# Router logits read out of the shared expert's product of rests

## The chip, the cores and the metric

The kernel runs on one core of one Trainium2 chip. The time is the device time of an execution in microseconds. A core has five engines with queues of their own: TensorE (PE in the profile, with its weight loads as PEld), VectorE (DVE), ScalarE (ACT), GpSimd (POOL) and SyncE (SP, used here to start DMAs). Each works through its own instructions in order; semaphores order them among each other. TensorE reads SBUF and writes PSUM, the accumulator memory, here in banks of 128 x 512 float32.

## The reference

One layer of a transformer over 64 batches of 128 tokens of 128 features: cross attention to 77 context tokens with 16 heads, then a feed-forward part with experts. Cut to what matters here:

```python
x = x + xattn(layernorm(x), ctx)              # 16 heads of 64, 77 keys
x2 = layernorm(x).reshape(-1, 128)            # 8192 tokens
logits = x2 @ router_w.T                      # 8 experts
_, idx = top_k(softmax(logits), 2)
gate = zeros; gate[token, idx] += logits[token, idx]
for e in range(8):
    h = silu(x2 @ w1[e].T) * (x2 @ w3[e].T)   # 176 wide
    moe_out += gate[:, e:e+1] * (h @ w2[e].T)
sh = silu(x2 @ sw1.T) * (x2 @ sw3.T)          # the shared expert, 176 wide
x = x + moe_out + sh @ sw2.T
```

All data are float32. The width 176 of an expert is worked as a main part of 128 and a "rest" of 48.

## The kernel before

The 64 batches are worked in 16 groups of 4 (512 tokens). Attention runs in units: one unit is one batch with 8 of the 16 heads, so a group has 8 units. The main loop over the 128 units issues for each: the scores of the unit two ahead (`ps`, whose two PSUM banks exist once, so the next scores wait until DVE has read the last: `mx`, `sc`), every second unit the output product `py`, then a list of work that is due at an even step, the transposes `pa` of this unit's attention weights, ACT's exponentials for the unit ahead, the values `pv`, a list due at an odd step, and last DVE's sums `sm`, `ri` and POOL's products `at`, which the transposes two units later read. Each unit thus has two steps and a group 16. Key products `pk` are due at each step. In odd groups of attention four products `pn` are due too, at steps 2, 4, 6 and 8.

The plan (`at(when, ...)`, lines 935 to 946) also places the routing of a group, in the 16 steps behind its attention: layer norm statistics at step 0, scaling at 1, transposing at 3 (`pxT_f`, copied by ACT to `x2T`), logits at 4, choice of the first expert at 5 and of the second at 6, places in the experts' lists at 8, and from 9 to 12 eight indirect DMAs by POOL that send the tokens (`sent`). A group's routing runs while the next group is in attention. "Odd" and "even" groups are those of the routing: while an even group is routed, an odd group is in attention, with `pn`.

For the first 13 groups (the last `LATE` = 3 are worked at the end) the shared expert stands in the same plan: up products of the main parts at step 11 (`p_s`, two products of 512 columns), the rest at 12, the down products at 14 (`pf`) and the storing at 17. The rest is one product, `ph_s`, of 112 weight columns: 0 to 47 are the first matrix, 64 to 111 the third, and 48 to 63 are zero. ACT takes a tanh of its first 48 rows, and DVE makes the gated rest `hr` of it in two instructions, `ur` and `hr`, that read the product in PSUM (lines 520 to 523).

Logits (lines 552 to 564) are four products, one a batch, of 128 weight columns (the batch's tokens in `x2T`) and 8 streamed columns (`rw_sb`), followed by a copy to SBUF on DVE, a maximum and a difference there, and an exponential on ACT. `choose` is nine small DVE instructions, `choose_second` seven with `sel`; `place` starts with products `pr` that read `sel`.

From step 160 on, the blocks of chosen tokens run between the units: sets of 9, 5 and 2 groups are sent and then worked in "quads" of four blocks, with copies of the experts' weights `w` on ACT and DVE, transposes `pt`, up products `p` and `ph`, down products `pq`, and indirect DMAs `answers`. Their gating uses the same functions, `gated` and `gated_rest`. PSUM banks other than those of the scores are six in a ring (`bank`). Every engine's instructions keep the order in which the recording layer leaves them.

Of the kernel before, what the change touches and what calls it, by code (L numbers as in the profile page):

```python
# [8 lines left out]
F32 = mybir.dt.float32  # L9
# [6 lines left out]
B, NQ, D = 64, 128, 128  # L16
# [10 lines left out]
E, I = 8, 176  # L27
IR = I - 128
HI = 64 + IR

W1, W3, WR, W2F, W2R, WALL = 0, 128, 256, 256 + HI, 384 + HI, 512 + HI
G = 4
NG = B // G

SETS = (9, 5, 2)

LATE = 3
# [8 lines left out]
def n_blocks(n):  # L46
    return 2 * n * G * NQ // 128 + E - 1

# [4 lines left out]

T = G * NQ
EPS = 1e-5
# [13 lines left out]
def xattn_moe_kernel(  # L69
# [9 lines left out]
    wvT: bass.AP,  # L79
    w_out: bass.AP,  # L80
    b_out: bass.AP,
    rwT: bass.AP,
    wx: bass.AP,
    wsh: bass.AP,
    out: bass.AP,
# [1 line left out]
    nc = tc.nc  # L87
    PSUM = bass.MemoryType.PSUM

    const = ctx.enter_context(tc.tile_pool(name="const", bufs=1))  # L90
# [8 lines left out]
    ffn = ctx.enter_context(tc.tile_pool(name="ffn", bufs=2))  # L99
    per_set = ctx.enter_context(tc.tile_pool(name="per_set", bufs=2))  # L100

    def weights_of(engine, w, q, n, name):

        to = ffn.tile([128, WALL], F32, tag="w", name=f"{name}_{q}", bufs=2 * QUAD)
        to = to[:, : 4 * n].rearrange("p (m d) -> p m d", d=n)
        engine.dma_start(out=to, in_=w[:, 4 * q : 4 * (q + 1), :])
        return to

    wk, wq, wv, wo = {}, {}, {}, {}
    for q in range(2):  # L110
        wq[q] = weights_of(nc.scalar, wqT, q, D, "wq")
        wk[q] = weights_of(nc.sync, wkT, q, DC, "wk")
    mhalf = const.tile([128, G], F32, name="mhalf")
    nc.gpsimd.memset(mhalf, -0.5)

    nc.scalar.activation(small.tile([128, G], F32, tag="shift", name="first_exp"), mhalf, AF.Exp)

    def load_keys(g):
        cT = grp.tile([DC, G, NKV], F32, tag="cT", name=f"cT_{g}", bufs=2)
        nc.sync.dma_start(out=cT, in_=ctxT[:, g * G : (g + 1) * G, :])  # L120
        return cT
# [30 lines left out]
        wv[q] = weights_of(nc.scalar, wvT, q, DC, "wv")  # L152
        wo[q] = weights_of(nc.sync, w_out, q, D, "wo")
    bo_sb = const.tile([128, D], F32, name="bo_sb")
    rw_sb = const.tile([D, E], F32, name="rw_sb")
    wsh_sb = const.tile([128, WALL], F32, name="wsh_sb")

    wx_sb = const.tile([128, E, WALL], F32, name="wx_sb")
    nc.scalar.dma_start(out=bo_sb, in_=b_out.rearrange("(o d) -> o d", o=1).broadcast_to([128, D]))
    nc.sync.dma_start(out=rw_sb, in_=rwT)  # L160
    nc.sync.dma_start(out=wsh_sb, in_=wsh)

    def load_expert(e):
# [6 lines left out]
    ident = const.tile([128, 128], F32, name="ident")  # L170
# [3 lines left out]
    for i in range(NAT):  # L174
        a = const.tile([128, 8 * (KM + KS)], F32, name=f"at_{i}")
# [60 lines left out]
    def bank(name, p=128):  # L236
        return ps_g.tile([128, 512], F32, tag="g", name=name)[:p]
# [230 lines left out]
    def wide(a, shape):  # L468

        return a.rearrange("p (b o) -> p b o", o=1).broadcast_to(shape)  # L470
# [17 lines left out]
    def gated(name, up, silu=False, n=T):  # L488

        p1 = bank(f"p1_{name}")  # L490
        up(p1, W1, 128)
        p3 = bank(f"p3_{name}")
        up(p3, W3, 128)
        a = ffn.tile([128, T], F32, tag="a", name=f"a_{name}")
        h = ffn.tile([128, T], F32, tag="h", name=f"h_{name}", bufs=3)
        of = slice(0, n)
        if silu:
            nc.scalar.activation(a[:, of], p1[:, of], AF.Silu)
            nc.vector.scalar_tensor_tensor(h[:, of], a[:, of], 2.0, p3[:, of], ALU.mult, ALU.mult)
        else:  # L500

            nc.scalar.activation(a[:, of], p1[:, of], AF.Tanh, scale=0.5)
            u = ffn.tile([128, T], F32, tag="u", name=f"u_{name}")
            nc.vector.scalar_tensor_tensor(u[:, of], a[:, of], 1.0, p1[:, of], ALU.add, ALU.mult)
            nc.vector.tensor_tensor(h[:, of], u[:, of], p3[:, of], ALU.mult)
        return h

    def gated_rest(name, up, silu=False, n=T):

        pr = bank(f"ph_{name}")  # L510
        up(pr, WR, HI)
        a = ffn.tile([128, T], F32, tag="a", name=f"ar_{name}")
        hr = hrs[hr_no[0] % NHR]
        hr_no[0] += 1
        of = slice(0, n)
        if silu:
            nc.scalar.activation(a[64:HI, of], pr[:IR, of], AF.Silu)
            nc.vector.scalar_tensor_tensor(hr[:IR, of], a[64:HI, of], 2.0, pr[64:HI, of], ALU.mult, ALU.mult)
        else:
            nc.scalar.activation(a[:IR, of], pr[:IR, of], AF.Tanh, scale=0.5)  # L520
            u = ffn.tile([128, T], F32, tag="u", name=f"ur_{name}")
            nc.vector.scalar_tensor_tensor(u[64:HI, of], a[:IR, of], 1.0, pr[:IR, of], ALU.add, ALU.mult)
            nc.vector.tensor_tensor(hr[:IR, of], u[64:HI, of], pr[64:HI, of], ALU.mult)  # L523
        return hr

    class Router:
# [23 lines left out]
            nc.scalar.copy(self.pay[:, 1, :, :D], self.pay[:, 0, :, :D])  # L550

        def logits(self):
            pl = bank(f"pl_{self.g}")
            for b in range(G):
                nc.tensor.matmul(
                    pl[:, b * E : (b + 1) * E], self.x2T[:, b * NQ : (b + 1) * NQ], rw_sb, start=True, stop=True
                )
            self.lg = lg = self.t3("lg")
            nc.vector.tensor_copy(lg.rearrange("p b e -> p (b e)"), pl[:, : G * E])
            m = self.t2("gm")  # L560
            nc.vector.tensor_reduce(m, lg, AX.X, ALU.max)
            self.sc = sc = self.t3("gsc")
            nc.vector.tensor_tensor(sc, lg, wide(m, sc.shape), ALU.subtract)
            nc.scalar.activation(sc, sc, AF.Exp)
# [90 lines left out]
        def up(self, to, c, m):  # L655
            nc.tensor.matmul(to[:m], wsh_sb[:, c : c + m], self.x2T, start=True, stop=True)  # L656

        def shared_up(self, silu=False):
            self.h = gated(f"s{self.g}", self.up, silu)
# [200 lines left out]
    def at(when, *steps):  # L860
        plan.setdefault(when, []).extend(steps)
# [42 lines left out]
    for g in range(NG):  # L904
        p = 16 * g
# [15 lines left out]
    def route(g, step, *args):  # L921
        if g not in routers:
            routers[g] = Router(g, next(s for s in sets if s.start <= g < s.start + s.n), atts[g].x1)
        getattr(routers[g], step)(*args)

    def routing(g, p, *steps):
        for k, step in steps:
            at(p + k, lambda step=step: route(g, step))

    g = 0  # L930
# [3 lines left out]
    assert g == NG  # L934
    for g in range(NG - 1):
        p = 16 * (g + 1)
        routing(g, p, (0, "stats"), (1, "normed"), (3, "transpose"), (4, "logits"), (5, "choose"), (6, "choose_second"))
    for st in sets:
        for g in range(st.start, min(st.start + st.n, NG - 1)):
            p = 16 * (g + 1)  # L940
            routing(g, p, (8, "place"))
            if g < NG - LATE:
                routing(g, p, (11, "shared_up"), (12, "shared_rest"), (14, "shared_down"), (17, "park"))
            for k in range(4):
                for c in range(2):
                    at(p + 9 + k, lambda g=g, c=c, b=k: routers[g].send(c, b))
    end = 16 * NG
    for st in sets[:-1]:
        p = 16 * (st.start + st.n)
# [6 lines left out]
    for st, after in zip(sets, sets[1:]):  # L956
# [4 lines left out]
        for q, quad in enumerate(quads):  # L961
            p = st.ready + (until - st.ready) * q // (len(quads) - 1)
# [109 lines left out]
    def unit(k):  # L1072
        g, b, t = units[k]
        return attention_of(g), b, t
# [28 lines left out]
    for k in range(len(units) + 1):  # L1103
# [3 lines left out]
        if k and k % 2 == 0:  # L1107
            a, b, t = unit(k - 1)
# [4 lines left out]
        a, b, t = unit(k)  # L1113
# [24 lines left out]
def _laid_out(inputs):  # L1138

    import numpy as np  # L1140

    a = {k: np.asarray(v) for k, v in inputs.items()}
    f = np.float32

    def packed(w1, w3, w2):

        w = np.zeros((128, WALL), f)
        w[:, W1:W3] = w1[:128].T
        w[:, W3:WR] = w3[:128].T
        w[:, WR : WR + IR] = w1[128:].T  # L1150
        w[:, WR + 64 : W2F] = w3[128:].T
        w[:, W2F:W2R] = w2[:, :128].T
        w[:IR, W2R:] = w2[:, 128:].T
        return w

    keys = a["ctx_768"].transpose(2, 0, 1)
    ctxR = np.zeros((DC, B, KS), f)
    ctxR[:, :, :KR] = keys[:, :, KM:]
    ctxM = keys[:, :, :KM].reshape(DC, B // 2, 2 * KM)
    ctxM = np.concatenate([ctxM, ctxM[:, :, :KM]], axis=2)  # L1160

    def by_pair(w):

        return w.reshape(NH // 2, 128, -1).transpose(1, 0, 2)

    w1, w2, w3 = (a[f"L0_ffn_w{n}"] for n in (1, 2, 3))
    return {
        "x": a["x"],
        "xT": a["x"].transpose(2, 0, 1),
        "ctxT": keys,  # L1170
        "ctxM": ctxM,
        "ctxR": ctxR,
        "wqT": by_pair(a["L0_xattn_w_q"].T),
        "wkT": by_pair(a["L0_xattn_w_kv"][:, :INNER].T),
        "wvT": by_pair(a["L0_xattn_w_kv"][:, INNER:].T),
        "w_out": by_pair(a["L0_xattn_w_out"]),
        "b_out": a["L0_xattn_b_out"],
        "rwT": a["L0_ffn_router_w"].T,
        "wx": np.concatenate([packed(w1[e], w3[e], w2[e]) for e in range(E)]),
        "wsh": packed(a["L0_ffn_sw1"], a["L0_ffn_sw3"], a["L0_ffn_sw2"]),  # L1180
    }


# [17 lines left out]
```

## Time and profile before

| what | us |
|---|---|
| median of 3 runs | 972.41 (971.56 to 974.22) |
| the profiled execution | 973.28 |
| its span | 971.6 |
| TensorE busy | 921.3 (95%) |
| VectorE busy | 668.8 (69%) |
| ScalarE busy | 653.0 (67%) |
| GpSimd busy | 520.2 (54%) |
| logits products, TensorE busy | 15.3 in 128 instructions |
| product of rests of the shared expert, TensorE busy | 16.4 in 32 instructions |

The span runs from the first to the last instruction of the profiled execution; 1.7 us lie around it. A product of float32 is recorded as two instructions, one a pass, and a transpose as one. Records of TensorE overlap[...]: what an instruction takes from the queue is read from the distance of two starts. In a group of instructions the line gives engine, operation, output and inputs with shapes, the count, then busy time in all and the mean of one in ns, then the idle time of the engine in front of them and what ended it. In the chain that ended last, each line is a start, a duration and the instruction.

### The profile page before, as it was taken

The numbers are of one execution on the slowest core, as the hardware profiler recorded it, in microseconds if no ns is written. First come the engines' busy times: TensorE is split into PE (matmuls) and PEld (weight loads), VectorE is DVE, ScalarE is ACT, GpSimd is POOL, SyncE is SP. The second block draws the span as 40 slices with busy tenths as digits, with TensorE's granted clock in tenths as the row PEclk, the third lists the DMA queues.
The fourth block names the chain that finished last, engine by engine and source line by source line (L and its number), as shares of the span: only waits on it lengthen the run. The fifth ranks groups of instructions, "written<-read, shape, count | busy, mean of one in ns | idle before, by whom it ended". The sixth has DMA issues, their size and how long they took to land.

```text
span 971.6 us, 18867 instructions
## 1 busy us (share of the span) xinstructions
PE 921.3 (95%) x6123; PEld 768.4 (79%) x6123; DVE 668.8 (69%) x1751; ACT 653.0 (67%) x1420; POOL 520.2 (54%) x688
## 2 busy tenths in 40 slices
PE   8999999999999999999999999999999988879794
PEld 7787878788778778787898878888888877779692
DVE  4566776777667667768787576777676787656464
ACT  5776667676767676676767685767766766576461
POOL 3244553636364636545457556475465483646773
PEclk9999999999999999999999999999999999999898
DMA  6222212222221232122403322221322032424886
GB/s 181 70 57 78 68 41 82 67 59 67 68 83 43 63 104 59 54 82 69 110 23 99 96 83 67 54 72 56 93 75 70 15 96 88 124 65 110 259 255 225
DMA packets 80882, 85.76 MB, mean 88 GB/s; under 512 B 11328, under 2 KB 62912, under 8 KB 80784
## 3 DMA queue, kind: packets, MB, share of 16 engines
q1 hardware_dynamic: 65920, 56.09, 21.4%
q0 software_dynamic: 8864, 18.30, 5.6%
q10 hardware_dynamic: 6000, 10.16, 2.9%
q8 instruction: 49, 0.80, 0.3%
q14 instruction: 49, 0.40, 0.1%
HBM read 48.18 MB, written 36.33 MB: 87 GB/s over the span
## 4 chain that ended last, share of the span: by engine, by line
PE 72%; DVE 10%; ACT 9%; DMA 4%; issue 3%; SPq 1%; ACTq 0%; POOL 0%; POOLq 0%; DVEq 0%
PE py L446 13%; PE ps L367 11%; PE pk L350 11%; PE pv L419 8%; PE pa L436 5%; PE p L784 5%; PE pn L456 2%; PE pq L797 2%; PE p_s L656 2%; PE pq L796 2%; PE ph L784 2%; DVE sm L389 1%; DVE sc L378 1%; ACT y L803 1%; PE pf L669 1%
## 5 line engine op out<-in xcount | busy, mean ns | idle before, releaser
L350 PEld LDWEIGHTS pk<-cT,wkq_sb 96*128 96x128 f32 x1024 | 157.9, 189 | 70.0 <-issue 42.8
L357 ACT COPY kx<-pk 128x308 f32<-128x308 f32 x256 | 104.3, 416 | 129.0 <-PE pk L350 123.5
L807 POOL DMA_INDIRECT answers<-y,to x149 | 149.4, 1003 | 72.4 <-ACT y L803 29.0
L350 PE MATMUL pk<-cT,wkq_sb 96*128 96x154 f32 x1024 | 175.0, 294 | 1.0 <-ACT wkq_sb L267 0.7
L446 PEld LDWEIGHTS py<-vo,aT 128*128 128x128 f32 x1280 | 154.7, 193 | 14.4 <-ACT vo L424 3.9
L367 PE MATMUL ps<-kx,xgT 128*128 128x308 f32 x512 | 156.7, 426 | 9.8 <-DVE sc L378 9.3
L446 PE MATMUL py<-vo,aT 128*128 128x128 f32 x1280 | 157.0, 277 | 3.0 <-ACT vo L424 2.6
L645 POOL DMA_INDIRECT sent<-pay,row x128 | 126.7, 989 | 61.5 <-DVE part L635 30.9
L399 POOL TENSOR_TENSOR at<-sc,ri 128x512 f32<-128x512 f32 x64 | 67.2, 1051 | 171.0 <-DVE ri L391 113.7
L424 ACT COPY vo<-pv 64x512 f32<-64x512 f32 x256 | 147.1, 574 | 2.1 <-ACT vn L464 0.4
L419 PE MATMUL pv<-wvo_sb,cM 96*128 96x512 f32 x256 | 131.2, 594 | 1.0 <-DVE hr L523 0.8
L389 DVE TENSOR_REDUCE sm<-sc 128x8 f32<-128x616 f32 x128 | 101.1, 790 | 40.1 <-ACT sc L382 39.2
L382 ACT ACTIVATE sc<-sc,rs_a 128x616 f32<-128x616 f32 x128 | 104.9, 820 | 25.9 <-DVE sc L378 16.9
L367 PEld LDWEIGHTS ps<-kx,xgT 128*128 128x128 f32 x512 | 88.9, 189 | 39.0 <-issue 8.9
L397 POOL TENSOR_TENSOR at<-sc,ri 128x256 f32<-128x256 f32 x128 | 76.8, 624 | 79.2 <-DVE ri L391 25.2
L439 ACT COPY aT<-pa 128x512 f32<-128x512 f32 (+1 forms) x256 | 96.1, 429 | 32.0 <-PE pa L436 27.3
L378 DVE TENSOR_TENSOR sc<-ps,mx 128x616 f32<-128x616 f32 x128 | 102.3, 800 | 12.5 <-POOL at L401 0.4
L376 DVE TENSOR_REDUCE mx<-ps 128x8 f32<-128x616 f32 x128 | 98.3, 768 | 7.7 <-PE ps L367 6.4
L436 PE MATMUL pa<-ident,at 128*128 128x128 f32 x640 | 91.7, 274 | 0.2 <-POOL at L397 0.2
L436 PEld LDWEIGHTS pa<-ident,at 128*128 128x128 f32 x640 | 75.2, 142 | 11.6 <-issue 10.7
L784 PE MATMUL p<-xT,w 128*128 128x128 f32 x596 | 75.2, 280 | 8.4 <-ACT xT L779 8.3
L784 PEld LDWEIGHTS p<-xT,w 128*128 128x128 f32 x596 | 71.0, 194 | 12.9 <-ACT xT L779 11.4
(152 smaller groups left out, 1402.6 us busy)
## 6 DMA issues: line engine op xcount, KB each, us to landing
xb<-sent SPq DMA_DIRECT2D x149, 65.0 KB
last_values<-vn ACTq DMA_DIRECT2D x32, 256.0 KB
vo<-last_values SPq DMA_DIRECT2D x64, 128.0 KB
ya<-answers SPq DMA_DIRECT2D x15, 512.0 KB
xgT<-in_xT_dram SPq DMA_DIRECT2D x16, 256.0 KB
xg<-in_x_dram SPq DMA_DIRECT2D x16, 256.0 KB
parked<-x SPq DMA_DIRECT2D x14, 256.0 KB
yx<-parked SPq DMA_DIRECT2D x14, 256.0 KB
```

Source lines behind the costliest of these rows:

```text
L350: nc.tensor.matmul(pk[:, k].rearrange("p (b k) -> p b k", k=NKV), wkq_sb[:, 2 * i + k, :], self.cT[:, 2 * p : 2 * (p + 1), :], start=True, ...
L367: nc.tensor.matmul(ps[:, r, : 4 * NKV].rearrange("p (j k) -> p j k", k=NKV), self.xgT[:, ts], self.kx[p][:, h : h + 4, ks], start=True, st ...
L378: nc.vector.tensor_tensor(at, sc, over_keys(mx), ALU.subtract)
L382: nc.scalar.activation(at, at, AF.Exp, scale=self.norm.rs[:, b : b + 1])
L389: nc.vector.tensor_reduce(sm, at, AX.X, ALU.add)
L419: nc.tensor.matmul(pv, self.cM[:, p, KM * r : KM * (r + 2)], wvo_sb[:, h : h + 4, :], start=True, stop=True)
L424: nc.scalar.copy(self.vo[b][rows, 4 * t : 4 * (t + 1), :], pv[rows].rearrange("p (m d) -> p m d", d=D))
L436: nc.tensor.transpose(pa[:, j * NQ : (j + 1) * NQ], keys[:, c : c + 128], ident)
L446: nc.tensor.matmul(py[:, :D], aT[:, m, :], vo[:, m, :], start=(m == 0), stop=(m == NT - 1))
L645: ins = nc.gpsimd.indirect_dma_start(out=sent[st.i], out_offset=bass.IndirectOffsetOnAxis(ap=self.row[:, i : i + 1], axis=0), in_=self.pay ...
L784: nc.tensor.matmul(to[:m, ts], self.w[j][:, c : c + m], self.xT[:, ts], start=True, stop=True)
L807: ins = nc.gpsimd.indirect_dma_start(out=answers[st.i], out_offset=bass.IndirectOffsetOnAxis(ap=self.to[:, j : j + 1], axis=0), in_=self.y ...
```

## The change

For the first 13 groups the logits come out of the shared expert's product of rests. The router's 8 weight columns are laid into the zero columns 48 to 55 of that product's weights, in the array `wsh` that the host lays out; the array `rwT` and its load go. The product `ph_s` moves from step 12 to step 4. ACT copies it whole, 112 x 512, from PSUM to a new SBUF tile `rests`. At step 5, four transposes of 128 tokens each turn the 112 rows into columns in one bank, and `weigh` (the rest of the former `logits`) reads columns 48 to 55 of each. `choose` moves from step 5 to 6 and `choose_second` from 6 to 7. At step 12 the tanh and the two DVE instructions read `rests` instead of the product in PSUM. For the last three groups logits are computed as before, with the weight columns from `wsh`. The tile `h` of the gating has two buffers instead of three.

```diff
+WG = WR + IR
...
-    rw_sb = const.tile([D, E], F32, name="rw_sb")
+    rests = const.tile([HI, T], F32, name="rests")
...
-    nc.sync.dma_start(out=rw_sb, in_=rwT)
...
-        h = ffn.tile([128, T], F32, tag="h", name=f"h_{name}", bufs=3)
+        h = ffn.tile([128, T], F32, tag="h", name=f"h_{name}", bufs=2)
...
     def gated_rest(name, up, silu=False, n=T):
-        pr = bank(f"ph_{name}")
-        up(pr, WR, HI)
+        if up is None:
+            pr = rests
+        else:
+            pr = bank(f"ph_{name}")
+            up(pr, WR, HI)
...
         def logits(self):
-            pl = bank(f"pl_{self.g}")
+            pl = bank(f"pl_{self.g}")[:, : G * E].rearrange("p (b e) -> p b e", e=E)
             for b in range(G):
                 nc.tensor.matmul(
-                    pl[:, b * E : (b + 1) * E], self.x2T[:, b * NQ : (b + 1) * NQ], rw_sb, start=True, stop=True
+                    pl[:, b, :], self.x2T[:, b * NQ : (b + 1) * NQ], wsh_sb[:, WG : WG + E], start=True, stop=True
                 )
+            self.weigh(pl)
+
+        def product_of_rests(self):
+            pr = bank(f"ph_s{self.g}")
+            self.up(pr, WR, HI)
+            nc.scalar.copy(rests, pr[:HI])
+
+        def logits_of_rests(self):
+            pl = bank(f"pl_{self.g}").rearrange("p (b e) -> p b e", b=G)
+            for b in range(G):
+                nc.tensor.transpose(pl[:, b, :HI], rests[:, b * NQ : (b + 1) * NQ], ident[:HI, :HI])
+            self.weigh(pl[:, :, IR : IR + E])
+
+        def gated_rests(self):
+            self.hr = gated_rest(f"s{self.g}", None)
+
+        def weigh(self, pl):
             self.lg = lg = self.t3("lg")
-            nc.vector.tensor_copy(lg.rearrange("p b e -> p (b e)"), pl[:, : G * E])
+            nc.vector.tensor_copy(lg, pl)
...
-        routing(g, p, (0, "stats"), (1, "normed"), (3, "transpose"), (4, "logits"), (5, "choose"), (6, "choose_second"))
+        routing(g, p, (0, "stats"), (1, "normed"), (3, "transpose"))
+        if g < NG - LATE:
+            routing(g, p, (4, "product_of_rests"), (5, "logits_of_rests"), (6, "choose"), (7, "choose_second"))
+        else:
+            routing(g, p, (4, "logits"), (5, "choose"), (6, "choose_second"))
...
-                routing(g, p, (11, "shared_up"), (12, "shared_rest"), (14, "shared_down"), (17, "park"))
+                routing(g, p, (11, "shared_up"), (12, "gated_rests"), (14, "shared_down"), (17, "park"))
...
+    shared = packed(a["L0_ffn_sw1"], a["L0_ffn_sw3"], a["L0_ffn_sw2"])
+    shared[:, WG : WG + E] = a["L0_ffn_router_w"].T
```

More of the change, by code (lines that the diff above doesn't have):

```diff
@@ L81, in xattn_moe_kernel @@
     b_out: bass.AP,
-    rwT: bass.AP,
     wx: bass.AP,
@@ L1177, in _laid_out @@
         "b_out": a["L0_xattn_b_out"],
-        "rwT": a["L0_ffn_router_w"].T,
         "wx": np.concatenate([packed(w1[e], w3[e], w2[e]) for e in range(E)]),
-        "wsh": packed(a["L0_ffn_sw1"], a["L0_ffn_sw3"], a["L0_ffn_sw2"]),
+        "wsh": shared,
     }
```

## The prediction

> **What bounds the kernel now.** First the page's head and the busy times, then the busy times of two stretches: attention and routing alone (50 to 430 us), and the stretch in which the experts' blocks run between attention units (columns: stretch, length, then busy us and instruction count of PE, PEld, DVE, ACT, POOL, granted clock, DMA share, GB/s).
>
> ```profile
> span 971.6 us, 18867 instructions
> ...
> PE 921.3 (95%) x6123; PEld 768.4 (79%) x6123; DVE 668.8 (69%) x1751; ACT 653.0 (67%) x1420; POOL 520.2 (54%) x688
> ```
>
> ```profile
> 50.00:430.00 380.00, 379.46 (x2328) 303.28 (x2327) 268.10 (x758) 264.85 (x571) 191.49 (x262) 1.00 0.22 65
> 480.00:850.00 370.00, 352.44 (x2463) 302.25 (x2462) 268.89 (x684) 253.24 (x563) 215.39 (x264) 1.00 0.26 75
> ```
>
> TensorE is the bound: 379.46 of 380 us at full clock, and 352 of 370 with experts. So what the change takes from TensorE's queue is a gain at its full issue time, unless another engine then makes TensorE wait. DVE is 71% busy and next. Third, the groups of instructions that the change removes or resembles (busy us, mean ns of one, then idle before and its releaser).
>
> ```profile
> L555 PE MATMUL pl<-rw_sb,x2T_f 128*128 128x8 f32 x128 | 15.3, 246 | 0.0
> L318 PE MATMUL pxT_f<-ident,pay 128*128 128x128 f32 x64 | 9.7, 274 | 0.0
> L320 ACT COPY x2T_f<-pxT_f 128x512 f32<-128x512 f32 x16 | 9.5, 591 | 0.0
> L564 ACT ACTIVATE gsc<-gsc 128x32 f32<-128x32 f32 x16 | 3.7, 230 | 24.7 <-DVE gsc L563 24.7
> ```
>
> Two things to see: the 64 logits products are 128 instructions (two passes each), the 64 transposes are 64 (one pass each); and ACT stands 24.7 us in all, 1.54 a time, in front of the router's exponential. Fourth, the chain that ended last, in order of time, over the router of group 3.
>
> ```profile
> 205.83 0.44 PE pxT_f L318 x4
> ...
> 210.25 0.81 PE pl L555 x8
> 211.09 0.20 DVE lg L559
> ...
> 213.80 0.19 DVE oh L574
> 213.99 0.71 DVE sm L389
> ...
> 215.70 0.80 DVE sc L378
> ...
> 216.65 1.28 PE ps L367 x4
> ...
> 231.82 0.86 PE ph_s L656 x2
> ```
>
> The four logits products hold TensorE for 0.81 us (the same distance, 0.81 to 0.82, stands behind all 16 of them in the timeline). Then, in this odd group, the chain leaves TensorE: logits, choice of the first expert, sm, mx, sc on DVE, and the next scores wait for sc. TensorE's previous product issued at 215.85 and takes 0.52, so it was ready at 216.37 and began at 216.65: 0.28 lost. Groups 1, 5 and 7 show 0.27 at the same place; even groups, which have an extra pn product there, lose nothing.
>
> **The change, part by part.** It touches 13 of the 16 groups.
>
> *1. Logits by transpose.* Removed: 4 products, 0.81 us. Added: 4 transposes of 112 columns. The nearest row is pxT_f, 4 transposes of 128 columns in 0.44; the five of pa take 0.54 (210.90 to about 211.45 in the timeline), the same 0.11 each. With 112 of 128 columns this is 0.38 if the streamed columns set the pace, 0.44 if the load of 128 columns does; I take 0.40. The Trainium skill ("TensorE: Matmul & The Clock Gate", Part 4: PE-mode transpose) speaks against this: it gives some 275 ns for one transpose in a kernel's context, so four would be 1.10 and the change would lose 0.29 x 13 = 3.8 us. The row has a mean of 274 ns too, but that is the length of one record: starts lie 0.11 apart because they overlap. I take the distance, so 13 x (0.81 - 0.40) = **-5.3** (4.8 to 5.6).
>
> *2. The product of rests (ph_s), 0.86 us, moves* from step 12 to step 4. It is not doubled, so the sum on TensorE is zero; between the steps the queue runs 0.86 + 0.40 - 0.81 = 0.45 later than before, afterwards 0.41 earlier. Its DMAs: none. The transposes wait for ACT's copy of it. Between product and transposes TensorE issues pa 0.54, pv 0.86 and pk 0.52 = 1.9 us; the copy (row x2T_f: 0.59, here 112 rows) needs about 0.15 + 0.59. Cover 1.2 us, and ACT is free there: it used to wait at this very place for the exponential. Where the cover is gone, TensorE stands for the difference, with the next scores behind.
>
> *3. ACT: 13 copies more*, 7.7 us busy. They fill the wait for the exponential, which moves to the end of the unit, behind aT, exp, vo and kx copies, by when DVE has its input. aT copies in group 3 begin at 211.75 instead of 211.90. Cost nothing; with ACT late, aT and kx would be late next, then py and scores. The tanh at step 12 no longer waits for ph_s (5.4 us in all by the waits), hidden, since DVE there has slack.
>
> *4. DVE: choose (9 small instructions, 2.0 us) moves a unit later*, so steps 4 and 5 carry 3 of them, steps 6 and 7 carry 16. Walk of group 3: transposes issue 212.88 to 213.28, lg at 213.47, gsc done 214.1, sm, ri, mx, sc to 216.61, next scores from 216.76; TensorE, 0.46 later, comes at 216.79. The 0.28 is then spent working: the odd groups gain it, 4 x 0.26 = **-1.0** (0 to -1.1). Then choose and second until 220.1, where pr needs sel at 220.66; sm, ri, mx, sc of the next unit to 222.65, wanted at 222.75. Margins of 0.5 and 0.1: that is the tight place. `place` comes at 222.9 instead of 220.84, so POOL's sends are 2.1 us later; its at tiles for units 6 and 7 are ready about 2.2 and 0.8 us before pa wants them. Even groups: pn's 0.86 gives slack, place is only 0.42 later.
>
> *5. Groups 9 to 12, between experts' blocks.* The exponential's waits there are 1.4 to 2.8 us of ACT; freeing them brings xT and the blocks' hr forward, and TensorE's waits just after the logits are 0.33, 0.35, 0.52 and 0.98 (xT or hr): of 2.2 I take **-1.0** (0 to -2.2). Against it, group 9: choose filled a DVE gap at 492.4 to 494.4; later it ends second at 504.2, and pr, at 503.4 in the queue, waits: **+0.85** (0 to 1.5).
>
> *6. The gate reads SBUF.* ur and hr now have two SBUF inputs (0.68 and 0.69, as before from PSUM). The skill ("SBUF — State Buffer", Who interferes with whom) says that such an instruction and a GpSimd instruction that reads SBUF exclude each other. This trace agrees: a pair of small products with two SBUF inputs, 0.29 elsewhere, took 1.59 under POOL's at.
>
> ```profile
> 504.68 1.59 DVE L623 SCALAR_TENSOR_TENSOR picked<-oh,place 128x32 f32<-128x32 f32 x2
> ```
>
> ```profile
> 504.83 1.06 POOL L399 TENSOR_TENSOR at<-sc,ri 128x512 f32<-128x512 f32 x1
> ```
>
> By the old row the two gates cost nothing; by the rule up to one at (0.62 to 1.06) each, 13 x 2 x 1.06 = 27 us if nothing hid it. In even groups POOL works on at and x through 279.1 to 281.9, where ur and hr run: about 0.9 later, hr done near 282.2, pf wants it at 282.35. In odd groups POOL is sending then. I take 0.05 a group, **+0.7** (0 to 4).
>
> *7. At nothing:* h in 2 buffers instead of 3 (no third up product stands ahead of the down product two blocks earlier in TensorE's order); one load less at the front of SP's queue; the router's columns inside wsh; banks (ph is freed after 0.75 us instead of 3).
>
> Sum: -5.3 - 1.0 - 1.0 + 0.85 + 0.7 = -5.75, say -5.8. The profiled execution took 973.28 (span 971.6, 1.7 around): 967.5. It lies 0.87 above the median of 972.41, so the forecast against the median is **966.6**.
>
> **Rivals.** (a) *DVE eats the gain.* Steps 6 and 7 hold 6.2 us of DVE (16 x 0.22, mx, sc, sm, ri) against a TensorE unit of some 4 us; if the margins 0.1 and 0.5 fall by 0.3 to 0.5, each group stalls that much at scores or pr: 13 x 0.4 = 5.2 given back, 971.8. For it: the margins; against it: the unit before is lighter by 2.0.
> (b) *Slower, by one mechanism: the gates of step 12 and POOL lock each other,* hr comes late at pf and sm, mx, sc behind it come late at scores. Each full at that DVE meets costs 1.06; with one per gate, 2.1 less a slack of some 0.5 leaves 1.6 x 13 = 20.8, less 6.45 (the sum without item 6) = +14.4: 986.8. It decides from 6.45/13 = 0.5 us a group for no change, 0.72 for 0.3% slower. For it: the 1.59 above. Against: sends, not at, lie there in odd groups. If it comes it is likelier near its point of decision, 976 to 980.
> (c) *The transposes are no cheaper* (two passes each, 0.8): 972.4 - 0.5 = 971.9. The x64 and x640 for 64 and 640 transposes speak against it.
>
> **Chances.** A change of 0.3% (2.9 us) is about what a measurement can tell. Main case 0.64 (own range 963.0 to 969.4), (a) 0.17, (b) 0.13, (c) 0.03, the rest (0.03) faster than 963 by more waits removed. So faster 0.67, same 0.20, slower 0.13. The range takes in the main case's bounds and (a) and (c) nearly whole: 962.5 to 974.5.
>
> **What would show it.** Right: 52 transposes pl, some 0.40 from the first to the next instruction; the exponential's wait on ACT near 5 us instead of 24.7; scores after step 5 of odd groups without a gap; TensorE's busy stretch unbroken to 430. Wrong: TensorE waiting for sel (pr), for sc (scores) or for hr (pf) in groups 0 to 8; ur or hr longer than 1 us; transposes 0.8 apart; new waits of POOL's at on DVE with pa behind them.

## The result and the profile after

The changed kernel takes 978.88 us (median of 6 runs, 977.14 to 981.29), the kernel before, run beside it, 972.86 (971.56 to 974.22): a ratio of 1.0054, 95% interval 1.004 to 1.0068. It is slower by 0.5%, where 966.6 (962.5 to 974.5) was forecast. Its profiled execution took 978.02.

The page's head and busy times of the changed kernel, and then its busy times in the two stretches that were shown of before:

```profile
span 976.3 us, 18778 instructions
...
PE 918.6 (94%) x6071; PEld 763.4 (78%) x6071; DVE 687.2 (70%) x1751; ACT 660.4 (68%) x1433; POOL 527.4 (54%) x688
```

```profile
50.00:430.00 380.00, 374.12 (x2273) 297.26 (x2271) 272.69 (x745) 265.26 (x569) 194.41 (x259) 1.00 0.22 65
480.00:850.00 370.00, 351.84 (x2438) 300.22 (x2436) 276.29 (x673) 258.90 (x572) 215.77 (x263) 1.00 0.26 75
```

TensorE's work fell by 2.7 us of record time, but from 50 to 430 us, where it had stood still for 0.54 us, it now stands still for 5.88. DVE is busy 18.4 us longer with the same number of instructions. Which ones, the groups of instructions say; first the gate's two in the kernel before, then those that the change added or altered:

```profile
L522 DVE SCALAR_TENSOR_TENSOR ur_s<-ar_s,ph_s 48x512 f32<-48x512 f32 x13 | 8.8, 681 | 5.3 <-ACT ar_s L520 5.2
L523 DVE TENSOR_TENSOR hr<-ur_s,ph_s 48x512 f32<-48x512 f32 x13 | 9.0, 690 | 0.4
```

```profile
L525 DVE SCALAR_TENSOR_TENSOR ur_s<-ar_s,rests 48x512 f32<-48x512 f32 x13 | 27.7, 2131 | 0.5
L526 DVE TENSOR_TENSOR hr<-ur_s,rests 48x512 f32<-48x512 f32 x13 | 13.9, 1072 | 0.4
L567 ACT COPY rests<-ph_s 112x512 f32<-112x512 f32 x13 | 7.6, 586 | 5.4 <-PE ph_s L677 5.4
L572 PE MATMUL pl<-ident,rests 112*128 112x112 f32 x52 | 7.1, 259 | 0.0
L585 ACT ACTIVATE gsc<-gsc 128x32 f32<-128x32 f32 x16 | 3.7, 232 | 7.3 <-DVE gsc L584 7.3
```

`ur_s` takes 2.13 us in the mean (0.70 at least, median 3.08, 3.42 at most) where it took 0.68, `hr` 1.07 where it took 0.69: together 23.8 us more in 13 groups, which is more than the whole rise of DVE. The transposes came out as forecast, and the exponential's wait nearly so (24.7 us before, 7.3 now, about 5 forecast). In the chain that ended last, group 3 now begins so:

```profile
215.48 0.40 PE pl L572 x4
215.88 0.02 issue
215.91 0.20 DVE lg L580
...
218.26 0.80 DVE sc L378
219.06 0.10 DVE gs L601
```

0.40 for the four transposes, where the four products held TensorE for 0.81. Now the gate of an even group (4) in the timelines of DVE, POOL and TensorE, in this order:

```profile
282.21 3.09 DVE L525 SCALAR_TENSOR_TENSOR ur_s<-ar_s,rests 48x512 f32<-48x512 f32 x1
285.34 0.69 DVE L526 TENSOR_TENSOR hr<-ur_s,rests 48x512 f32<-48x512 f32 x1
```

```profile
282.01 1.20 POOL L397 TENSOR_TENSOR at<-sc,ri 128x256 f32<-128x256 f32 x2
283.16 0.38 POOL L401 TENSOR_TENSOR at<-sc,ri 128x104 f32<-128x104 f32 x1
283.49 1.26 POOL L339 TENSOR_TENSOR x<-xg,bo_sb 128x512 f32<-128x512 f32 x1
284.91 1.28 POOL L666 DMA_INDIRECT sent<-pay,row  x1 [0.16 <-issue]
```

```profile
284.47 0.39 PE L689 MATMUL pf<-wsh_sb,h_s 128*128 128x128 f32 x2
286.08 0.49 PE L690 MATMUL pf<-wsh_sb,hr 128*128 128x128 f32 x2 [1.22 <-DVE hr L526]
```

POOL began 0.2 us earlier, and its four products and sums follow each other without a gap until 284.75. `ur_s` ends at 285.30, which is 0.55 behind the last of them: DVE stood through the whole run, not through one instruction (this standing is called the lock below), and the down product `pf` waits 1.22 us for `hr`. Beside the indirect DMA `sent`, which POOL issues next, `hr` takes its usual 0.69.

Where the time went along the kernel is read from the starts of the 128 scores `ps` in TensorE's timeline: start before minus start after, so positive is gained. The last column is an experiment told below, in which only the gate's lock is taken away.

| stretch of before | changed kernel | with the gate by way of PSUM |
|---|---|---|
| groups 0 to 7, to 429.92 us | -4.12 | +3.74 |
| group 8, to 482.20 | -2.44 | -2.30 |
| group 9, to 550.19 | -2.30 | -1.23 |
| groups 10 to 12 and the rest, to 828.22 | +2.87 | +3.27 |
| sum | -5.99 | +3.48 |

The stretches don't make up the whole span: ahead of the first score the changed kernel loses 0.2 us, and behind the last one it gains 1.5 (the version with PSUM 1.7). What gains there is open.

By steps, the even groups 0, 2, 4 and 6 of the changed kernel lose 0.40 at steps 4 and 5, gain 0.86 at step 12 and then lose 1.47 to 1.65 at `pf`. The odd groups lose 0.40, gain 0.26 behind the logits and 0.62 at step 12, and lose 0.44 at the gate.

### The profile page after: what moved, and what is told of

Same layout as the page of the kernel before. It is cut to its first block, busy times and chain, and to the rows that moved or that the text cites. A ratio compares the mean times of both kernels' runs of the same rounds, so it can differ in the third digit from the quotient of the medians.

```text
span 976.3 us, 18778 instructions
## 1 busy us (share of the span) xinstructions
PE 918.6 (94%) x6071; PEld 763.4 (78%) x6071; DVE 687.2 (70%) x1751; ACT 660.4 (68%) x1433; POOL 527.4 (54%) x688
## 4 chain that ended last, share of the span: by engine, by line
PE 59%; DVE 20%; ACT 9%; DMA 5%; issue 4%; POOL 2%; SPq 1%; ACTq 1%; DVEq 0%; POOLq 0%
PE py L446 10%; PE pk L350 9%; PE ps L367 8%; PE pv L419 7%; PE pa L436 4%; PE p L805 4%; DVE sc L378 3%; DVE sm L389 3%; PE pn L456 3%; PE pq L818 3%; DVE mx L376 3%; PE pq L817 2%; DVE ur_s L525 2%; ACT vo L424 2%; ACT sc L382 2%
## 5 line engine op out<-in xcount | busy, mean ns | idle before, releaser
L666 POOL DMA_INDIRECT sent<-pay,row x128 | 130.0, 1016 | 53.4 <-issue 24.4
L397 POOL TENSOR_TENSOR at<-sc,ri 128x256 f32<-128x256 f32 x128 | 79.8, 647 | 79.3 <-DVE ri L391 25.2
```

The lines of the kernel that those rows point to most:

```text
L666: ins = nc.gpsimd.indirect_dma_start(out=sent[st.i], out_offset=bass.IndirectOffsetOnAxis(ap=self.row[:, i : i + 1], axis=0), in_=self.pay ...
```

## The experiments

### The gate without its second SBUF input

```diff
-        a = ffn.tile([128, T], F32, tag="a", name=f"ar_{name}")
+        a = None if up is None else ffn.tile([128, T], F32, tag="a", name=f"ar_{name}")
...
+            room = bank(f"gr_{name}") if up is None else None
+            a = a if room is None else room
...
-            u = ffn.tile([128, T], F32, tag="u", name=f"ur_{name}")
+            u = ffn.tile([128, T], F32, tag="u", name=f"ur_{name}") if room is None else room
```

The tanh and `u` of the gate lie in a PSUM bank (the "PSUM room" below); all else is the changed kernel.

> The changed kernel, but the tanh's result and u of the shared gate of rests lie in a PSUM bank, so that ur and hr each have one SBUF input (the rests) and one PSUM input. Everything else, the early logits, the ACT copy and the late choice, is as in the changed kernel. Theory of the lock (DVE instructions with two SBUF inputs stand while GpSimd works): ur_s falls from a mean of 3.08 us to about 0.7 us, TensorE's wait for hr at pf goes, and the time falls by the some 15 us that the stage differences put on the lock: 963 to 967 us. Rival (DVE is bunched at steps 6 and 7 and eats the gain there): nothing changes there, 977 to 980 us.

(The 3.08 named there is the median; the mean is 2.13.) Measured: 969.59 us (968.08 to 970.6), ratio to before 0.9966 (0.9954 to 0.9979). The groups of the two gates, whose outputs are now called after the bank:

```profile
L527 DVE SCALAR_TENSOR_TENSOR gr_s<-gr_s,rests 48x512 f32<-48x512 f32 x13 | 9.0, 692 | 0.1
L528 DVE TENSOR_TENSOR hr<-gr_s,rests 48x512 f32<-48x512 f32 x13 | 9.0, 693 | 0.4
```

Each gate is back at 0.69, no even group's `pf` waits, and 9.3 us of the median are gone (9.47 by the starts of the scores). The same data, the same engines and the same order: the lock is the cause of the loss. But 963 to 967 had been expected, and some 3 us are missing. The last column of the table puts most of them in group 8, and the odd groups lack a little each; both are taken up below. Rival (a), DVE bunched by the late choice, cannot be what made the kernel slow, since the late choice is still there.

### The kernel before with the lock alone

```diff
-        h = ffn.tile([128, T], F32, tag="h", name=f"h_{name}", bufs=3)
+        h = ffn.tile([128, T], F32, tag="h", name=f"h_{name}", bufs=2)
...
+        if copied:
+            nc.scalar.copy(rests, pr[:HI])
+            pr = rests
```

> The kernel before with only the gate's input changed: at step 12 ACT copies ph_s into SBUF and ur and hr of the shared expert read that copy; logits and choice stay where they were. Theory of the lock: ur_s has a mean of 2 us or more, pf waits for hr in most groups, and the time rises to 978 to 986 us (13 groups by 0.5 to 1.1 us; the copy makes the gate 0.6 us later too). Rival (the loss comes from the late choice): the time stays at 972 to 974 us and ur_s below 1 us.

Measured: 978.59 us (977.67 to 979.99), ratio 1.0058 (1.0038 to 1.0078).

```profile
L526 DVE SCALAR_TENSOR_TENSOR ur_s<-ar_s,rests 48x512 f32<-48x512 f32 x13 | 26.1, 2011 | 12.0 <-ACT ar_s L524 12.0
L527 DVE TENSOR_TENSOR hr<-ur_s,rests 48x512 f32<-48x512 f32 x13 | 10.2, 784 | 0.4
```

With logits and choice untouched, reading the copy costs 5.7 us. By the starts of the scores groups 0 to 7 lose 0.55 to 0.71 each, groups 8 and 10 lose 1.1 and 0.7, and groups 9, 11 and 12 nothing. It is less than 9.3 because the copy and then the tanh come later here, so that POOL's run is further gone when DVE begins: in group 4 it had begun 1.39 us earlier, against 0.20 in the changed kernel. The delay by the copy is not what costs there: with the lengths of the kernel before `hr` would be done at 284.4 (an estimate), and `pf` stood ready for it from 285.38 to 285.66.

### POOL's run shortened

The changed kernel, lock and all, with POOL's residual `x` two steps later:

```diff
-            at(p + 12, lambda g=g: residual(g + 1))
+            at(p + 14, lambda g=g: residual(g + 1))
```

> The changed kernel with one of GpSimd's instructions, the residual x of 1.27 us, moved two steps later, from step 12 to step 14, so that GpSimd's unbroken run under the gate is one instruction shorter. If DVE stands until the whole run of GpSimd is over: in even groups ur_s falls from 3.08 to about 1.8 us, pf no longer waits there (it waits 1.2 us), and the time falls to 971 to 973 us. If DVE stood for one instruction only (0.6 to 1.2 us), ur_s would stay as it is, and so would the time, 977 to 980 us.

Measured: 968.97 us (965.93 to 972.1), ratio 0.9955 (0.9937 to 0.9974). The even group 4 in the timelines of DVE and then POOL:

```profile
278.91 1.52 DVE L525 SCALAR_TENSOR_TENSOR ur_s<-ar_s,rests 48x512 f32<-48x512 f32 x1
280.46 0.74 DVE L526 TENSOR_TENSOR hr<-ur_s,rests 48x512 f32<-48x512 f32 x1
```

```profile
278.67 1.20 POOL L397 TENSOR_TENSOR at<-sc,ri 128x256 f32<-128x256 f32 x2
279.82 0.85 POOL L401 TENSOR_TENSOR at<-sc,ri 128x104 f32<-128x104 f32 x1
280.82 1.27 POOL L666 DMA_INDIRECT sent<-pay,row  x1
```

One POOL instruction of 1.27 us less behind the gate, and `ur_s` is 1.57 us shorter (3.09 to 1.52). That DVE waits for more than the instruction it meets is so confirmed: the `x` that went stood two instructions behind. That it waits for the whole run is not: here DVE got in after the first two products, and it was POOL's third that stretched, from 0.38 to 0.85. What decides between them after each instruction, no run shows. The time is better than the 971 to 973 expected. By the starts of the scores groups 0 to 7 get 6.1 us back: 1.52 already fits into the slack in front of `pf`, so that groups 2, 4 and 6 lose nothing there, while the odd ones still lose 0.40 to 0.43. Another 1.3 us come at one place near 790 us, from another instruction (next section).

### Both cures together

```diff
+            room = bank(f"gr_{name}") if up is None else None
...
-            at(p + 12, lambda g=g: residual(g + 1))
+            at(p + 14, lambda g=g: residual(g + 1))
```

> Both cures of the lock at once: the PSUM room for the gate, and the residual x two steps later. If both act on the same thing (ur and hr standing under GpSimd's run), they don't add up: 968 to 970 us, as each alone (969.6 and 969.0). If the later residual helps in another way too, its gain comes on top: 960 to 963 us.

Measured: 967.63 us (966.11 to 967.92), ratio 0.9939 (0.9922 to 0.9955), the fastest version run. The two cures don't add up: up to group 7 the scores gain 3.68 us over their start, against 3.74 with the PSUM room alone, so the later residual gives nothing there once the lock is gone. The 2 us between the two medians are slightly more than "the same" would allow. In the profiled executions the clock at group 8 makes 1.64 us of difference (below) and one more lock 1.3, while 0.8 are lost ahead of the first score. The kernel before has that lock too: one of the small DVE instructions `to`, with two SBUF inputs and 0.16 us long in the median of 38, stood 2.43 us under three of POOL's products and the residual (791.02 to 793.76), and the scores behind it waited 1.12 us for `sc`. The kernel before, and then the one with both cures:

```profile
791.36 2.43 DVE L800 TENSOR_TENSOR to<-xb,block_row 128x3 int32<-128x3 f32 x1
```

```profile
786.28 0.90 DVE L823 TENSOR_TENSOR to<-xb,block_row 128x3 int32<-128x3 f32 x1
```

With the later residual, here and in the section above, these scores come 1.3 us sooner. That gain belongs to the place of the residual and not to the change; the kernel before with the later residual alone was not run.

### The gate in DVE's idle time

DVE stands 2.9 us in front of `u_s` at step 11. Two attempts, both with the PSUM room (the diffs show only what else they change), put the gate there:

```diff
-(11, "shared_up"), (12, "gated_rests"), (14, "shared_down"), (17, "park")
+(11, "gated_rests"), (11, "shared_up"), (14, "shared_down"), (17, "park")
```

> The gate by way of PSUM as in the run with the PSUM room, and the gate of rests moved from step 12 to step 11, ahead of the shared expert's up products, where DVE stands idle for 2 to 3 us. Theory of the lock: as with the PSUM room alone or a little better, since hr is done earlier and u_s finds DVE free: 963 to 966 us. Rival (bunching at steps 6 and 7): 977 to 980 us.

Measured: 982.7 us (981.76 to 986.47), ratio 1.0112 (1.0082 to 1.0142); both expectations were wrong. DVE's timeline in group 3:

```profile
231.66 0.70 DVE L527 SCALAR_TENSOR_TENSOR gr_s<-gr_s,rests 48x512 f32<-48x512 f32 x1 [2.93 <-ACT gr_s L525]
232.39 0.69 DVE L528 TENSOR_TENSOR hr<-gr_s,rests 48x512 f32<-48x512 f32 x1
233.11 0.69 DVE L504 SCALAR_TENSOR_TENSOR u_s<-a_s,p_s 128x512 f32<-128x512 f32 x1
```

The gate's tanh was issued at step 11 too, so ACT took it at 231.03, behind exponential, `vo` and `kx`. DVE, in order, stood 2.93 us in front of the gate instead of in front of `u_s`, and the gate's 1.4 us came on top; the next scores waited 1.52 us for `sc`. The second attempt issues the tanh a step earlier:

```diff
+(10, "tanh_of_rests"), (11, "gated_rests"), (11, "shared_up"), (14, "shared_down"), (17, "park")
```

> As with the PSUM room, but the gate's tanh is issued at step 10 and ur and hr at step 11 ahead of u_s, in the 2.9 us in which DVE stands idle before u_s in the trace. The earlier attempt at step 11 had the tanh behind ACT's kx copy, so that DVE stood 2.9 us in front of ur with u_s behind it. Theory: ur now comes right behind sc of step 10 with no idle time before it, u_s keeps its time, DVE is 1.4 us lighter at step 12, and odd groups get back the 0.10 us that scores still wait there: 968.5 to 970 us. If instead what cost 13 us in that attempt was the two DVE instructions as such and not where their tanh stood, the time stays near 982 us.

Measured: 971.87 us (968.81 to 973.66), ratio 0.9984 (0.9972 to 0.9997). The 13 us of the first attempt are gone, so it was the tanh's place and not the two instructions. The first gate now starts at 225.62, right behind `sc` (224.91, 0.80 long), and the wait in front of `u_s` falls to 1.54. But nothing is gained on the version with the gate at step 12: an odd group gains 0.67 at step 12 and loses 0.07 behind it, against 0.71 and 0.10. In both, `u_s` starts when ACT delivers `a_s`, and `u_s`, `h_s`, `sm`, `ri`, `mx` and `sc` follow without a gap. With the gate at step 12 `sc` ends at 232.43 in group 3, the scores start at 232.49, and TensorE had been free for them from 232.34; with the gate at step 11 it is 232.57, 232.72 and 232.53. So 0.15 to 0.19 us of the odd groups stay at this chain, wherever the gate is. The median lies 1.9 us above what was expected; in its profile TensorE runs two stretches of 3.41 us at half clock behind group 8.

### The choice at its old steps

The kernel with the PSUM room and the early logits, but with the choice where it was before the change:

```diff
-(4, "product_of_rests"), (5, "logits_of_rests"), (6, "choose"), (7, "choose_second")
+(4, "product_of_rests"), (5, "logits_of_rests"), (5, "choose"), (6, "choose_second")
```

> The kernel with the PSUM room for the gate (969.6 us), but choose and choose_second back at steps 5 and 6, as before the change; the logits stay early. By item 4 of the prediction the four odd groups lose their 0.26 us a unit after step 5 (scores wait for sc again), and group 9 no longer waits 0.8 us for sel: together nothing that a median shows, 969 to 971 us. If the late choice bunches DVE (rival a), the time falls instead, by some 0.2 to 0.4 us a group, to 965 to 967 us.

Measured: 997.16 us (996.74 to 1002.96), ratio 1.0238 (1.0221 to 1.0255): 27.6 us slower than with the late choice, a clear miss. DVE's timeline in group 3, and the row of TensorE's waits:

```profile
223.13 0.19 DVE L582 COPY lg<-pl 128x32 f32<-128x32 f32 x1 [3.41 <-PE pl L574]
...
224.42 0.19 DVE L603 TENSOR_REDUCE gs<-gsc 128x4 f32<-128x32 f32 x1 [0.65 <-ACT gsc L587]
...
228.10 0.80 DVE L378 TENSOR_TENSOR sc<-ps,mx 128x616 f32<-128x616 f32 x1
```

```profile
PE ps L367 <- DVE grest L615: 18.2, 9, 2.4
```

Before, the logits started 2.8 us ahead of the scores that follow them in TensorE's queue (210.09 and 212.87); the transposes start 0.4 ahead (222.54 and 222.93). DVE sits 3.41 us in front of `lg`, and with `choose` in the same step nine more instructions and the wait for the exponential come between `lg` and the next `sc`: scores 2.43 us late in this group. The row has these waits of groups 0 to 8, 18.2 us in all, put down to `grest`, the instruction right behind `sc`. They bring a second loss with them: TensorE has six stretches at half clock between 126 and 420 us, 23.9 us in all, where the version with the late choice has none. So the late choice is no tax on the early logits but what makes them possible. Item 4 had priced the move against the old logits only.

### Group 8 and the clock

In the kernel with the PSUM room group 8 loses 2.30 us, 1.66 of it between two scores. Its busy times there, in steps of 3.41 us from the clock's own edges (columns as before; behind POOL's stands the granted clock):

```profile
453.01:456.43 3.42, 2.46 (x20) 2.06 (x18) 3.28 (x7) 1.57 (x4) 2.96 (x4) 1.00 0.52 115
456.43:459.84 3.41, 1.66 (x7) 0.94 (x7) 3.17 (x7) 0.03 (x1) 1.51 (x4) 1.00 0.58 181
459.84:463.25 3.41, 3.41 (x9) 2.71 (x10) 3.22 (x6) 2.24 (x4) 3.22 (x5) 0.50 0.05 17
```

and the kernel with both cures, at the same place:

```profile
454.83:458.25 3.42, 2.35 (x14) 1.46 (x13) 3.18 (x9) 1.57 (x4) 2.42 (x3) 1.00 0.56 115
458.25:461.66 3.41, 1.76 (x9) 1.30 (x9) 3.24 (x7) 0.94 (x2) 1.92 (x4) 1.00 0.38 139
461.66:465.07 3.41, 3.41 (x28) 3.21 (x27) 3.21 (x6) 1.88 (x5) 2.22 (x4) 1.00 0.08 24
```

TensorE stands still for 2.7 us in both, since DVE works out the tables of the first set there; in the first it then gets half the clock for 3.41 us (9 instructions instead of 28), in the second not. Only one execution of each version was profiled; the granted clock of all its runs is 0.987 in the median for both versions, against 0.988 for the kernel before, so how often the clock falls at this place is not known. Two ways to shorten the stall were tried. The tables in two parts, the first a step earlier:

```diff
-        at(p + 10, lambda st=st: tables(st))
+        at(p + 9, lambda st=st: tables(st))
+        at(p + 10, lambda st=st: rest_of_tables(st))
```

> As with the PSUM room, but the first seven DVE instructions of the tables (2.4 us with the matmul's wait) are issued a step earlier, at step 9, so that DVE is less late at the end of group 8. In the profiled run with the PSUM room TensorE was idle for 1.75 of the 3.41 us from 456.4 to 459.8 and then had half its clock for 3.41 us (1.7 us lost); before the change the idle time there was cut in two (0.64 and 1.15 in windows of 3.41 us) and the clock stayed whole. Theory: with less idle time in that stretch the clock stays whole and the waits shrink by about 1 us: 966 to 968 us, granted clock 1.00 throughout 450 to 480 us. Rival: the half clock there is chance, or comes from elsewhere, and the time stays at 969 to 970 us.

Measured: 970.85 us (968.99 to 971.51), ratio 0.9967 (0.9954 to 0.9979): no gain, two stretches at half clock. TensorE's stalls there were 0.21, 0.87 and 1.47 us. And the shared expert of group 8 two steps later, on both versions:

```diff
+                d = 2 * (g == sets[0].n - 1)
+                routing(g, p, (11 + d, "shared_up"), (12 + d, "gated_rests"), (14 + d, "shared_down"), (17 + d, "park"))
```

> As with the PSUM room and the later residual (967.6 us), but in group 8 alone, behind whose routing DVE works out the tables of the first set, the shared expert's steps come two steps later, so that its four DVE instructions (2.8 us) no longer stand between the tables and the scores. In the profiled runs TensorE is idle for about 2.7 us in that stretch and in most of them then runs 3.41 to 6.83 us at half clock. Theory: the idle time there falls by 2 us or more, no stretch of 3.41 us is idle by half any more, the granted clock stays 1.00 from 440 to 490 us, and the time falls to 964 to 966 us. Rival: DVE is bound by the tables themselves, the wait only moves to the next scores, and the time stays at 967 to 969 us.

> The same change of group 8 on the kernel with the PSUM room alone (969.6 us), whose profiled run shows the half clock for 3.41 us there. Theory: 2 us less waiting and the 1.7 us of the half clock go, 965 to 967 us, clock 1.00 from 440 to 490 us. Rival: the wait only moves, 969 to 970 us.

In these runs the kernel before itself took 1018.48 us, why is not known, so only the ratios tell something: 0.9988 (0.9972 to 1.0004) with both cures, 0.9989 (0.997 to 1.0009) with the PSUM room; medians 1016.36 and 1017.44. No gain shows, and the traces say why: the scores of step 12 come 1.7 us sooner than with both cures, but two units later scores wait 2.06 us for `sc`, because `u_s` and `h_s` now stand there, and the 1.7 are gone; at the end of group 8 the scores are 2.0 us behind those of the same version without this move. The rival was right, the wait moves. The two kernels have the same stall (2.06 and 2.07 us), cut differently by the clock's steps; the first row is the step with most of it, the second the step behind, with both cures:

```profile
464.56:467.97 3.41, 1.95 (x12) 1.66 (x13) 2.92 (x5) 1.88 (x4) 2.60 (x3) 1.00 0.49 114
467.97:471.39 3.42, 3.42 (x33) 3.42 (x32) 3.25 (x8) 2.04 (x4) 1.39 (x2) 1.00 0.19 60
```

and with the PSUM room alone:

```profile
462.31:465.73 3.42, 1.35 (x7) 0.81 (x6) 3.28 (x6) 0.76 (x3) 1.38 (x2) 1.00 0.03 6
465.73:469.14 3.41, 3.41 (x11) 2.71 (x12) 2.96 (x7) 3.37 (x6) 0.00 (x0) 0.50 0.42 99
```

## Why the prediction was wrong

The step that failed is **item 6, the gate that reads SBUF**: booked at +0.7 us (0 to 4), it cost 9.3, the distance between the changed kernel and the one whose gate has a PSUM input. The mechanism was the one named there and in rival (b); its size was worked out from a wrong picture. That working let DVE meet one POOL instruction of at most 1.06 us per gate, found the even groups' gate "about 0.9 later", done just when `pf` wants it, and the odd groups free. The trace of before held the run of four back-to-back POOL instructions (279.1 to 281.9) that item 6 itself quotes; in the changed kernel DVE stood through all of it, 2.4 us more than the 0.69 it needs. That a run counts and not one instruction could be read there too, from the `to` of 2.43 us at 791.36, which the working did not look at. In the odd groups POOL was not only sending: its two `at` products and the gate stretch each other (`ur_s` 0.97, `hr` 0.99, the products 2.03 instead of 1.20 at 236.46 to 238.93). That is 1.5 us an even group and 0.44 an odd one, 7.9 in groups 0 to 7. Over the 13 groups it is 9.3 / 13 = 0.72, just what rival (b) had asked for a kernel slower by 0.3%; it became 0.5% because the rest of the sum gave less. The rival's likely outcome, 976 to 980, came.

The rest of the sum, -6.45, was measured by itself with the PSUM room: -3.3 by the medians.

- Item 1, the transposes: right, 0.40 for four (even groups gain 0.44 each, 0.41 forecast), against the 1.10 that the record's length would have made. Rival (c) falls.
- Item 2, the moved product: the 0.45 (measured 0.40) and its return at step 12 came in full in the even groups (0.86). In the odd groups only 0.71 came back and the next scores lost 0.10, so that they gain 0.50 each in place of 0.67: with `ph_s` gone from in front of them, the scores wait for `sc`. The prediction named no work that this product had been covering; it covered DVE's chain from `u_s` to `sc`.
- Item 3, ACT's copies at nothing: nothing on TensorE's path waits for them in groups 0 to 8.
- Item 4: the 0.26 in odd groups came where it was forecast, and was given back at step 12 (item 2). The tight margins held: no wait for `sel` in groups 0 to 8.
- Item 5: group 9's wait of `pr` behind the later choice came, but as 0.43 us in the waits (0.85 forecast); with what follows at `pa` and `pv` the scores lose 0.94 there. (The 0.8 of `pr` for `sel` in the list of waits is the last group's and stands in the kernel before too.) Groups 9 to 12 together gained 2.04 us with the PSUM room, where 4 x 0.41 + 1.0 - 0.85 = 1.8 were forecast.
- Group 8 was no item. TensorE's gain there is worth nothing, since DVE's tables set its pace, and the profiled execution lost 1.66 more to the clock: -2.30 in place of +0.41, nearly all that is missing by the starts of the scores (+3.48 of 6.45).
- Item 7, nothing for the buffers of `h`, the load and the banks: TensorE's waits name none of them.

Rival (a) was not what made the kernel slow. It is right so far as DVE gives back some 0.25 us in each odd group, at step 12 and not at steps 6 and 7.

With its own lock out of the way the change gives about half of what was forecast without item 6: 969.59 us. The 967.63 with both cures, close to the forecast, has the residual's own 1.3 us in it and, in its profiled execution, a clock that stayed whole at group 8; that it meets the forecast is in part luck.

## What to carry to other kernels

Before an operand moves from PSUM to SBUF, count the SBUF inputs of the DVE instructions that read it: with two, they stand behind GpSimd's products and sums, and the price is up to the unbroken run of them at that place in the timeline, not one of them; a PSUM bank for the other operand takes it away. (The bank may have a price of its own: in groups 9 and 11 the versions with it at step 12 get back 0.05 to 0.06 and 0.58 us there, where the version with the later residual alone gets 0.71 and 0.86. Why, no run shows.) When an instruction leaves a stage of the bound engine, look for the chain on the next engine that it had been covering there. And where an in-order engine has idle time, an instruction fits into it only if its own input is there when the idle time begins.

## What was not expected of the hardware

**The lock outlasts an instruction.** The Trainium skill ("SBUF — State Buffer", SBUF: two separate sides) lets whichever of the two engines starts first hold the SBUF ports that they share for the whole instruction. Here a DVE instruction of 0.69 us took 3.09, across the boundaries of four POOL instructions, and in another kernel got in after two of them while POOL's next took 0.85 for 0.38. Nor does starting first protect it: in the odd groups `ur_s` began at 236.46, POOL's products at 236.90, and both were stretched.

**A stall of 2 us can cost twice.** The granted clock changes in steps of 3.41 us. In the profiled executions it fell to 0.50 behind the stall of group 8 with steps in which TensorE was busy 1.19, 1.66 and 1.35 us of 3.41 (the changed kernel, the PSUM room, group 8 later), and stayed whole with 1.76, 1.95 and 2.31 (both cures, group 8 later with both cures, the kernel before). The kernels with the PSUM room alone and with both cures have equal stalls, before and after group 8 was altered, so where the steps' edges fall may decide over 1.7 us; no run moved the edges alone. The skill ("TensorE: Matmul & The Clock Gate", Part 1: The HAM clock gate) calls this window free-running, which fits. How long TensorE is busy in one step does not decide by itself: with the tables in two parts a step with 1.88 us busy was followed by half clock, and with the choice at its old steps one of 1.72 us (from 178.36) was, while another of 1.71 (from 82.79) was not. The prediction had taken the clock of before as given.
